# A graph layer with routed experts: other set sizes, a mean taken from a product's own sum, and a bias added as one row on TensorE

## The chip, the core and the metric

The kernel runs on one core of a Trainium2 chip. A core has five engines that run in parallel, each in the order of its own program: TensorE (PE in the profile; its weight loads are the row PEld), VectorE (DVE), ScalarE (ACT), GpSimd (POOL) and SyncE (SP). Sixteen DMA engines move data between the main memory and the on-chip memory; here SP issues the plain transfers and POOL the indirect ones, which gather or scatter rows by an index. The metric is the device time of one execution in microseconds; lower is better.

## The reference

One layer over 6,250 nodes with 256 features and 100,000 edges, all in float32:

```python
xn = _layernorm(x, axis=-1)
x = x + gnn(xn, edges, W, b, gamma, beta) + mix(xn, Wq, Wkv, Wproj, bproj)
x = x + ffn(_layernorm(x, axis=-1), gate_w, gate_b, w1, b1, w2, b2, gamma, beta)
```

`gnn` is a graph convolution: rows of `x @ W` are summed over edges with weights, normalised, and combined with its input. `mix` is linear attention with eight heads. `ffn` is a mixture of 16 experts, of which each node uses two; this is the part that the change touches:

```python
topk_vals, topk_idx = jax.lax.top_k(x @ gate_w + gate_b, 2)
topk_w = jax.nn.softmax(topk_vals, axis=-1)
h = relu(einsum('bsh,ehf->bsef', x, w1) + b1)          # 256 -> 512
expert_out = einsum('bsef,efh->bseh', h, w2) + b2      # 512 -> 256
y = x + sum(topk_w * take_along_axis(expert_out, topk_idx))
mu = mean(y); var = var(y)
return (y - mu) / sqrt(var + EPS) * gamma + beta
```

## The kernel before, in words

Nodes lie in 49 tiles of 128 (the last has 106). One long loop goes over the 782 chunks of 128 edges, a "slot" each. In a slot POOL gathers 128 rows by index (L1163), DVE writes a matrix that places them (L1167), and six slots later PE multiplies the two and so sums the edges of a tile (L1176, sums taken up at L1185). Everything else is woven into these slots by hand: `Weave` keeps pieces, Python generators, each with the slot of its next step; a step emits its instructions, and `yield n` puts the next step n slots later. The slot numbers thus fix the order of the instructions on every engine; time does not enter. After the last slot the pieces go on in the same order.

Once a pair of tiles has all its edges, `residual` makes the new `x` and the gate's logits. Tiles then go to the experts in phases, listed in `SETS` (L118): two sets, of 36 and 13 tiles, each cut into phases that end at the tile numbers given. After a phase `route` finds a slot in an expert's blocks for each token, and `scatter` lets POOL write the token's row there (L911, two per tile). A block is 128 tokens of one expert. In all but the last phase of a set only full blocks are worked on; the number that a phase counts on is a constant (`hi`, two blocks a tile less a margin), and at the set's last phase, its flush, it is `USUAL`. If the counts of the data do not bear out these constants, a flag makes the kernel do the whole expert part again (after L1194).

`expert` (L942) is one block: SP loads the first weights and the tokens, five slots later the second weights, the first bias (512 values) and the second bias `b2`, which lies in memory as a copy of 256 values for each of the 128 partitions (L965); after four more slots PE turns the tokens (L973) and ACT copies them (L977, "the xT copy"); then PE's first product (L981) and its copy to the on-chip memory (L985, "the h copy", on DVE, but on ACT in the last flush), PE's four turns (L989), ACT's four relus (L994), PE's second product `yp` (L998), DVE's addition of `b2` (L1002), and SP's store. Blocks of the first set follow each other by 8, 6 and, in its flush, 5 slots, those of the second by 4. There are four places for weights.

`combine` (L1012) works on two tiles: POOL gathers the two experts' rows of each (L1025) and ACT normalises `x` into `y` (L1029); six slots later DVE adds the two weighted rows (L1036, two products a tile) and takes mean and variance (`stats`, L312 and L313); then ACT's root and DVE's reciprocal (L318, L319), and for each tile two products and a sum give the output (L1044, L1045, L1047), which SP stores. The first set's pairs begin when its last block is stored, five slots apart; the second set's when the last block of all is stored.

Of the kernel before, what the change touches and what calls it, by code (L numbers as in the profile page):

```python
# [23 lines left out]
F32 = mybir.dt.float32  # L24
# [3 lines left out]
AF = mybir.ActivationFunctionType  # L28
OP = mybir.AluOpType
AX = mybir.AxisListType  # L30

P = 128
N = 6250
D = 256
NT = (N + P - 1) // P
# [16 lines left out]
FJ = F // P  # L52
KB = (2 * N + NE * (BLK - 1)) // BLK
WROW = 2 * F + FJ * D + FJ + D


def rows(t):
    return min(P, N - t * P)
# [56 lines left out]

SETS = ((8, 12, 16, 20, 24, 28, 32, 36), (42, 46, NT))  # L118
CUT = SETS[0][-1]
USUAL = [2 * CUT + 11, 2 * (NT - CUT) + 12]  # L120
MOST = [(2 * n + NE * (P - 1)) // P for n in (CUT * P, N - CUT * P)]
# [2 lines left out]
WA = 2 * F  # L124
# [112 lines left out]
def windowed_layer(ctx: ExitStack, tc: tile.TileContext, X, rows3, ident, loc_t, w_t, W, b, gamma, beta, wqT, wkvT, wprojT, bproj,  # L237
# [71 lines left out]
    def stats(pool, mv, src_tile):  # L309
        r = src_tile.shape[0]  # L310
        st = pool.tile([P, 6], F32, name="bnst", bufs=4)
        v.bn_stats(st[:r], src_tile)  # L312
        v.bn_aggr(mv, st[:r])  # L313

    def inv_std(pool, rs, var):
        sd = pool.tile([P, rs.shape[1]], F32, name="sd", bufs=2)
        p = rs.shape[0]
        act(sd[:p], var, AF.Sqrt, bias=eps_t[:p], scale=1.0)  # L318
        v.reciprocal(rs, sd[:p])  # L319
# [618 lines left out]
    def sync(to, source):  # L938
        issued[0] = nc.sync.dma_start(to, source).ins
        return issued[0]  # L940

    def expert(z, n, j, homes, bank, gap, copy_h):  # L942

        def row(i):
            if not loaded.get((z, i)):
                _, regs = nc.values_load_multi_w_load_instructions(
                    states[z]["rows"][0:1, i, j:min(j // 8 * 8 + 8, ends[z, j])], engines=[mybir.EngineType.SP],
                    min_val=0, max_val=(MOST[z] if i == 0 else NE - 1) * P,
                    skip_runtime_bounds_check_because="bounded by a minimum where it is computed")
                loaded[z, i] = list(regs)  # L950
            return loaded[z, i].pop(0)

        at, slots = row(1), row(0)
        wp_ = homes["w"].take()
        w = wp_()[:, :WROW]
        sync(w[:, :WA], experts[bass.ds(at, P), :WA])
        xp = homes["x"].take()
        xs = xp()
        i = sync(xs, xslots[z][bass.ds(slots, P), :])
        if n is not None:  # L960
            for m in range(n + 1, len(SETS[z])):
                tc.declare_no_dep(i, group=f"tokens{z}_{m}", reason="a full block takes no more tokens")
            tc.add_to_no_dep_group(f"loads{z}", i)
        yield gap[0]
        sync(w[:, WA:], experts[bass.ds(at, P), WA:])  # L965
        w1 = w[:, :WA].rearrange("p (c f) -> p c f", c=2)
        w2 = w[:, WA:WA + FJ * D].rearrange("p (j d) -> p j d", j=FJ)
        b1 = w[:, WA + FJ * D:WA + FJ * D + FJ]
        b2 = w[:, WROW - D:]
        yield gap[1]  # L970
        tp = bank("xtp").rearrange("p (k c) -> p k c", k=4)
        for c in range(2):
            nc.tensor.transpose(tp[:, c, :], xs[:, c * P:(c + 1) * P], ident)  # L973
        homes["x"].give(xp)
        xTp = homes["xT"].take()
        xT = xTp().rearrange("p (k c) -> p k c", k=2)
        nc.scalar.copy(xT, tp[:, :2, :])  # L977
        yield 2
        hp = bank("hp")
        for c in range(2):  # L980
            nc.tensor.matmul(hp, xT[:, c, :], w1[:, c, :], start=(c == 0), stop=(c == 1))  # L981
        homes["xT"].give(xTp)
        h_ = homes["h"].take()
        h = h_()
        copy_h(h, hp)  # L985
        yield 3
        tp = bank("htp").rearrange("p (k c) -> p k c", k=4)
        for f in range(FJ):
            nc.tensor.transpose(tp[:, f, :], h[:, f * P:(f + 1) * P], ident)  # L989
        homes["h"].give(h_)  # L990
        hTp = homes["hT"].take()
        hT = hTp().rearrange("p (k c) -> p k c", k=FJ)
        for f in range(FJ):
            act(hT[:, f, :], tp[:, f, :], AF.Relu, bias=b1[:, f:f + 1], scale=1.0)  # L994
        yield 2
        yp = bank("yp")
        for f in range(FJ):
            nc.tensor.matmul(yp[:, :D], hT[:, f, :], w2[:, f, :], start=(f == 0), stop=(f == FJ - 1))  # L998
        homes["hT"].give(hTp)
        y_ = homes["y"].take()  # L1000
        y = y_()
        v.tensor_add(y, yp[:, :D], b2)  # L1002
        homes["w"].give(wp_)
        yield 2
        before_it = issued[0]
        i = sync(yslots[z][bass.ds(slots, P), :], y)
        if n is not None:
            tc.declare_no_dep(i, group=f"stores{z}", reason="every block has rows of its own", keep=[before_it])
            tc.add_to_no_dep_group(f"stores{z}", i)
        homes["y"].give(y_)  # L1010

    def combine(ts_, homes, pool, last):  # L1012

        n = len(ts_)
        mv = pool.tile([P, n, 2], F32, name="mv", bufs=3)
        rs = pool.tile([P, n], F32, name="rs", bufs=3)
        v.memset(mv, 1.0)
        both = pool.tile([P, 2, D], F32, name="xn2", bufs=3)
        got, ys = {}, []
        for i, t in enumerate(ts_):  # L1020
            r = rows(t)
            z = 0 if t < CUT else 1
            for k in range(2):
                got[i, k] = homes["got"].take()
                nc.gpsimd.indirect_dma_start(  # L1025
                    out=got[i, k]()[:r], out_offset=None, in_=yslots[z],
                    in_offset=IndirectOffsetOnAxis(ap=slot_i[:r, t, k:k + 1], axis=0))
            y = both[:, i, :]
            act(y[:r], X[:r, t, :], AF.Identity, bias=nm2[:r, t:t + 1], scale=rs2[:r, t:t + 1])  # L1029
            ys.append(y)  # L1030
            yield 1
        yield 4
        for i, t in enumerate(ts_):
            r, y = rows(t), ys[i]
            for k in range(2):
                v.scalar_tensor_tensor(y[:r], got[i, k]()[:r], w12[:r, t, k:k + 1], y[:r], op0=OP.mult, op1=OP.add)  # L1036
                homes["got"].give(got[i, k])
            stats(pool, mv[:r, i, :], y[:r])
            yield 2
        inv_std(pool, rs, mv[:, :, 1])  # L1040
        yield 1
        for i, t in enumerate(ts_):
            r, y = rows(t), ys[i]
            v.scalar_tensor_tensor(y[:r], y[:r], mv[:r, i, 0:1], last[:r, 0, :], op0=OP.subtract, op1=OP.mult)  # L1044
            v.scalar_tensor_tensor(y[:r], y[:r], rs[:r, i:i + 1], last[:r, 1, :], op0=OP.mult, op1=OP.add)  # L1045
            o = pool.tile([P, D], F32, name="row", bufs=3)
            v.tensor_add(o[:r], y[:r], X[:r, t, :])  # L1047
            sync(out[t * P:t * P + r, :], o[:r])
            yield 2
# [59 lines left out]
    for z, phases in enumerate(SETS):  # L1109
        lo = 0  # L1110
        for n, b in enumerate(phases):
            flush = n == len(phases) - 1
            for t0 in range(a, b, 2):
                t1 = min(b, t0 + 2)
                at = max(at, min(NCH, 16 * t1 + 4) + LAG + 3)
                weave.add(at, residual(range(t0, t1)))
                last_at = at
                for t in range(t0, t1):
                    summed_at[t] = at + 3
                    if t + RING < NT and t >= 4:  # L1120
                        sum_from(t + RING)
                at += 10
            hi = USUAL[z] if flush else max(0, 2 * (b - CUT * z) - 11)
            ready = max(last_at + RES, scattered - 2)
            weave.add(ready, route(z, a, b, lo, hi, n == 0, flush))
            if flush:
                weave.add(ready + 6, token_weights(CUT * z, b))
            slow = 0 if z and flush else 1
            weave.add(ready + 2, scatter(z, n, a, b, 9, "token" if slow else "got", slow))
            scattered = ready + 11 + 2 * (b - a) * slow  # L1130
            ready += 14 + (2 * (b - a) * slow)
            for j in range(lo, hi):
                ends[z, j] = hi
                block = max(block + (4 if z else 8 if n < 3 else 5 if flush else 6), ready)
                weave.add(block, expert(z, n, j, homes, bank, (4, 3) if n < 3 and z == 0 else (5, 4),
                                        nc.scalar.copy if z and flush else v.tensor_copy))
            lo, a = hi, b
        if z == 0:
            ready_a = block + 18
# [574 lines left out]
```

## Time and profile before

| | |
|---|---|
| median of 3 runs | 1546.07 us (1545.3 to 1546.55) |
| profiled execution | 1549.07 us |
| its span, from first to last instruction | 1547.3 us |
| PE busy | 1312.2 us (85%) |
| DVE busy | 975.0 us (63%) |
| POOL busy | 967.1 us (63%) |
| ACT busy | 530.6 us (34%) |
| moved by DMA | 367.32 MB, mean 237 GB/s |

Where stretches of the span are listed, a line holds the stretch and its length, then for each engine the busy time and, in brackets, its instructions, then the granted clock of PE (1.00 is full), the mean busy share of the DMA engines, and what they moved. A line of the order of time holds start and busy time, engine, line of the code, operation, names (out<-in), sizes, and in square brackets the idle time before it and what ended that. A line of one group of instructions holds minimum, median and maximum duration in ns. The line numbers are those of the kernel before.

### The profile page before, as it was taken

To read this page: it belongs to the slowest core of one execution; us is meant where nothing else is said; L and a number is where in the kernel's file an instruction comes from. 1 tells how busy PE (TensorE), PEld (TensorE's weight loads), DVE (VectorE), ACT (ScalarE), POOL (GpSimd) and SP (SyncE) were. 2 spreads that over 40 slices of the span, in tenths; PEclk is the share of its full clock that TensorE was granted. 3 is DMA by queue.
4 is the path that set the end of the run, shared out by engine and by line. 5 is a ranking of instruction groups with operands and counts; after the bars stand their busy time and mean duration, and the time that the engine had idled before them with its cause. 6 is when DMAs were issued, how large, how long until landed. Compare 5 with 4: busy or idle time off the path is not lost. (4 is left out here: it accounts for less than half of the span.)

```text
span 1547.3 us, 22816 instructions
## 1 busy us (share of the span) xinstructions
PE 1312.2 (85%) x6144; PEld 930.1 (60%) x6144; DVE 975.0 (63%) x3338; ACT 530.6 (34%) x1417; POOL 967.1 (63%) x999
## 2 busy tenths in 40 slices
PE   4879999988768889898998989979999998788930
PEld 3836666666545567565776766757766765455620
DVE  8754444368855756757667676755565576989245
ACT  3653444423231223222332232323232335455420
POOL 1017777777777777777777777777667734753042
PEclk9999999999868989999999999999999999899975
DMA  9789933333345766677887878768878868899932
GB/s 279 260 271 376 371 103 99 103 97 115 102 159 169 242 221 224 222 258 254 275 280 234 275 258 283 233 236 287 284 241 288 289 201 317 308 378 368 361 102 70
DMA packets 180841, 367.32 MB, mean 237 GB/s; under 512 B 27091, under 2 KB 118152, under 8 KB 180694
## 3 DMA queue, kind: packets, MB, share of 16 engines
q1 hardware_dynamic: 132746, 236.69, 44.1%
q0 software_dynamic: 47712, 128.17, 26.0%
q8 instruction: 55, 0.90, 0.2%
q10 hardware_dynamic: 236, 0.80, 0.2%
q14 instruction: 92, 0.75, 0.2%
HBM read 290.00 MB, written 75.54 MB: 236 GB/s over the span
## 5 line engine op out<-in xcount | busy, mean ns | idle before, releaser
L1163 POOL DMA_INDIRECT rows<-w_hs,src_t x782 | 762.2, 975 | 354.1 <-ACT two_a L552 89.7
L1176 PE MATMUL acc<-rows,hot 128*128 128x256 f32 x1564 | 443.6, 396 | 37.4 <-DMA rows<-w_hs,src_t 31.1
L1176 PEld LDWEIGHTS acc<-rows,hot 128*128 128x128 f32 x1564 | 278.9, 195 | 129.4 <-issue 60.6
L1167 DVE TENSOR_SCALAR hot<-iota_g,loc_t,w_t 128x128 f32<-128x128 f32 x782 | 245.1, 354 | 4.0 <-PE acc L1176 4.0
L1025 POOL DMA_INDIRECT Q<-w_yslots,slot_i x98 | 99.4, 1015 | 141.8 <-issue 81.1
L994 ACT ACTIVATE hT<-htp,early 128x128 f32<-128x128 f32 x296 | 84.5, 368 | 205.6 <-issue 130.1
L998 PE MATMUL yp<-early,hT 128*128 128x256 f32 x592 | 148.2, 396 | 5.2 <-ACT hT L994 5.2
L981 PE MATMUL hp<-early,Q 128*128 128x512 f32 x296 | 143.2, 607 | 5.6 <-ACT Q L977 4.7
L998 PEld LDWEIGHTS yp<-early,hT 128*128 128x128 f32 x592 | 116.9, 198 | 32.7 <-ACT hT L994 10.8
L985 DVE COPY Q<-hp 128x512 f32<-128x512 f32 x92 | 63.4, 689 | 113.7 <-PE hp L981 113.0
L911 POOL DMA_INDIRECT w_xslots<-Q,slot_i x98 | 99.6, 1016 | 46.8 <-issue 37.1
L555 DVE SCALAR_TENSOR_TENSOR row<-two_a,two_b 128x256 f32<-128x256 f32 (+1 forms) x49 | 21.0, 430 | 132.0 <-ACT two_b L553 132.0
L549 PE MATMUL kq<-early,xnT 128*128 128x512 f32 (+1 forms) x196 | 98.5, 627 | 4.3 <-ACT xnT L545 4.3
L981 PE MATMUL hp<-Q 128*128 128x512 f32 x188 | 92.4, 615 | 10.1 <-ACT Q L977 9.1
L989 PE MATMUL htp<-ident,Q 128*128 128x128 f32 x484 | 74.7, 278 | 21.4 <-DVE Q L985 17.8
L998 PE MATMUL yp<-Q,hT 128*128 128x256 f32 x376 | 91.6, 388 | 0.4 <-ACT hT L994 0.3
L1002 DVE TENSOR_TENSOR Q<-yp,early 128x256 f32<-128x256 f32 x74 | 31.3, 423 | 95.6 <-PE yp L998 88.2
L318 ACT ACTIVATE sd<-mv,eps_t 128x2 f32<-128x2 f32 (+2 forms) x76 | 22.8, 300 | 195.5 <-DVE mv L313 191.5
L994 ACT ACTIVATE hT<-htp,Q 128x128 f32<-128x128 f32 x188 | 53.5, 367 | 94.7 <-issue 77.6
L981 PEld LDWEIGHTS hp<-early,Q 128*128 128x128 f32 x296 | 55.6, 193 | 49.1 <-issue 36.2
L998 PEld LDWEIGHTS yp<-Q,hT 128*128 128x128 f32 x376 | 72.9, 195 | 19.6 <-ACT hT L994 5.2
L1185 DVE SCALAR_TENSOR_TENSOR agg<-acc,dinv,agg 64x256 f32<-64x256 f32 x135 | 65.0, 482 | 28.6 <-PE acc L1176 25.9
(266 smaller groups left out, 1933.0 us busy)
## 6 DMA issues: line engine op xcount, KB each, us to landing
early<-in_experts SPq DMA_DIRECT2D x74, 642.0 KB
early<-in_experts SPq DMA_DIRECT2D x74, 512.0 KB
Q<-in_experts SPq DMA_DIRECT2D x47, 642.0 KB
Q<-in_experts SPq DMA_DIRECT2D x47, 512.0 KB
w_xslots<-zero_b SPq DMA_DIRECT2D x16, 1024.0 KB
w_yslots<-zero_b SPq DMA_DIRECT2D x16, 1024.0 KB
Q<-w_xslots SPq DMA_DIRECT2D x121, 128.0 KB
w_yslots<-Q SPq DMA_DIRECT2D x121, 128.0 KB
```

The source lines that it names most:

```text
L549: nc.tensor.matmul(kq[:r], xnT[:, k, :r], wkq[:, k, :], start=(k == 0), stop=(k == 1))
L911: i = nc.gpsimd.indirect_dma_start(out=xslots[z], out_offset=IndirectOffsetOnAxis(ap=slot_i[:r, t, k:k + 1], axis=0), in_=y[:r], in_offset ...
L981: nc.tensor.matmul(hp, xT[:, c, :], w1[:, c, :], start=(c == 0), stop=(c == 1))
L985: copy_h(h, hp)
L989: nc.tensor.transpose(tp[:, f, :], h[:, f * P:(f + 1) * P], ident)
L994: act(hT[:, f, :], tp[:, f, :], AF.Relu, bias=b1[:, f:f + 1], scale=1.0)
L998: nc.tensor.matmul(yp[:, :D], hT[:, f, :], w2[:, f, :], start=(f == 0), stop=(f == FJ - 1))
L1025: nc.gpsimd.indirect_dma_start(out=got[i, k]()[:r], out_offset=None, in_=yslots[z], in_offset=IndirectOffsetOnAxis(ap=slot_i[:r, t, k:k + ...
L1163: nc.gpsimd.indirect_dma_start(out=hrows[c], out_offset=None, in_=hs, in_offset=IndirectOffsetOnAxis(ap=src_t[:, c:c + 1], axis=0))
L1167: v.tensor_scalar(hots[c], iota_g[:, group_of(c) % 2, :], loc_t[:, c:c + 1], w_t[:, c:c + 1], op0=OP.is_equal, op1=OP.mult)
L1176: nc.tensor.matmul(accs[g], hots.pop(c), hrows.pop(c), start=begin, stop=end)
L1185: v.scalar_tensor_tensor(agg(t)[p0:p1], acc[p0:p1, :], dinv[p0:p1, t:t + 1], agg(t)[p0:p1], op0=OP.mult, op1=OP.add)
```

## The change

There are three edits.

The sets become 40 tiles in nine phases and 9 tiles in two, instead of 36 in eight and 13 in three. The number of blocks provided follows: 91 and 30 instead of 83 and 38, 121 in all both times. In the second set the first phase's margin grows by one, so that it counts on no block.

In the blocks of the second set only one row of `b2` is loaded, by a transfer of its own, and PE adds it to `yp` by a product of one row of ones with that row. DVE's addition becomes a copy.

In `combine` DVE's second product of a tile also writes the sum of its result. DVE scales the two sums of a pair to minus the mean; ACT takes the squares of `y` plus that, with their sum, into the place of the gathered rows; ACT's root and DVE's reciprocal follow, and the output adds minus the mean where it subtracted the mean. The statistics of DVE go, and so does the filling of `mv` with ones except for the tile that is not full.

```diff
-SETS = ((8, 12, 16, 20, 24, 28, 32, 36), (42, 46, NT))
+SETS = ((8, 12, 16, 20, 24, 28, 32, 36, 40), (46, NT))
...
-        sync(w[:, WA:], experts[bass.ds(at, P), WA:])
+        if row_b2:
+            sync(w[:, WA:WROW - D], experts[bass.ds(at, P), WA:WROW - D])
+            sync(w[0:1, WROW - D:], experts[bass.ds(at, 1), WROW - D:])
+        else:
+            sync(w[:, WA:], experts[bass.ds(at, P), WA:])
...
-            nc.tensor.matmul(yp[:, :D], hT[:, f, :], w2[:, f, :], start=(f == 0), stop=(f == FJ - 1))
+            nc.tensor.matmul(yp[:, :D], hT[:, f, :], w2[:, f, :], start=(f == 0), stop=(not row_b2 and f == FJ - 1))
+        if row_b2:
+            nc.tensor.matmul(yp[:, :D], ones[0:1, :], b2[0:1, :], start=False, stop=True)
...
-        v.tensor_add(y, yp[:, :D], b2)
+        if row_b2:
+            v.tensor_copy(y, yp[:, :D])
+        else:
+            v.tensor_add(y, yp[:, :D], b2)
...
+        minus, squares = mv[:, :, 0], mv[:, :, 1]
...
-        v.memset(mv, 1.0)
+        if rows(ts_[-1]) < P:
+            v.memset(mv, 0.0)
...
-            for k in range(2):
-                v.scalar_tensor_tensor(y[:r], got[i, k]()[:r], w12[:r, t, k:k + 1], y[:r], op0=OP.mult, op1=OP.add)
-                homes["got"].give(got[i, k])
-            stats(pool, mv[:r, i, :], y[:r])
-            yield 2
-        inv_std(pool, rs, mv[:, :, 1])
+            v.scalar_tensor_tensor(y[:r], got[i, 0]()[:r], w12[:r, t, 0:1], y[:r], op0=OP.mult, op1=OP.add)
+            v.scalar_tensor_tensor(y[:r], got[i, 1]()[:r], w12[:r, t, 1:2], y[:r], op0=OP.mult, op1=OP.add,
+                                   accum_out=minus[:r, i:i + 1])
+            homes["got"].give(got[i, 0])
+            yield 1
+        v.tensor_scalar(minus, minus, -1.0 / D, None, op0=OP.mult)
+        for i, t in enumerate(ts_):
+            r = rows(t)
+            act(got[i, 1]()[:r], ys[i][:r], AF.Square, bias=minus[:r, i:i + 1], accum_out=squares[:r, i:i + 1])
+            homes["got"].give(got[i, 1])
         yield 1
+        sd = pool.tile([P, n], F32, name="sd", bufs=2)
+        act(sd, squares, AF.Sqrt, bias=eps_t, scale=1.0 / D)
+        yield 1
+        v.reciprocal(rs, sd)
         for i, t in enumerate(ts_):
             r, y = rows(t), ys[i]
-            v.scalar_tensor_tensor(y[:r], y[:r], mv[:r, i, 0:1], last[:r, 0, :], op0=OP.subtract, op1=OP.mult)
+            v.scalar_tensor_tensor(y[:r], y[:r], minus[:r, i:i + 1], last[:r, 0, :], op0=OP.add, op1=OP.mult)
...
-            hi = USUAL[z] if flush else max(0, 2 * (b - CUT * z) - 11)
+            hi = USUAL[z] if flush else max(0, 2 * (b - CUT * z) - 11 - z)
...
                 weave.add(block, expert(z, n, j, homes, bank, (4, 3) if n < 3 and z == 0 else (5, 4),
-                                        nc.scalar.copy if z and flush else v.tensor_copy))
+                                        nc.scalar.copy if z and flush else v.tensor_copy, z == 1))
```

More of the change, by code (lines that the diff above doesn't have):

```diff
@@ L940, in sync, with expert @@
         return issued[0]
-    def expert(z, n, j, homes, bank, gap, copy_h):
+    def expert(z, n, j, homes, bank, gap, copy_h, row_b2=False):
         def row(i):
```

## The prediction

> **What bounds the kernel now.** I read the page's slices first, to see which engine is full when; then busy times by stretch, cut at events of the trace; then the order of time of VectorE (DVE), TensorE (PE) and ScalarE (ACT) inside a stretch.
>
> ```profile
> core 0: us, PE busy (x) PEld busy (x) DVE busy (x) ACT busy (x) POOL busy (x), PEclk, DMA share, GB/s
> 1035.90:1259.90 224.00, 214.06 (x965) 158.82 (x966) 132.44 (x428) 67.95 (x201) 144.35 (x149) 0.98 0.81 275
> 1259.90:1302.40 42.50, 39.09 (x178) 25.96 (x177) 26.14 (x96) 18.39 (x55) 18.32 (x19) 1.00 0.73 260
> 1375.50:1402.60 27.10, 24.16 (x91) 15.47 (x90) 24.73 (x70) 14.89 (x44) 16.48 (x16) 0.94 1.03 384
> 1433.50:1484.60 51.10, 49.35 (x203) 32.73 (x202) 8.75 (x24) 25.67 (x74) 0.00 (x0) 1.00 0.79 285
> 1490.00:1533.80 43.80, 0.00 (x0) 0.00 (x0) 37.59 (x104) 6.60 (x16) 24.82 (x24) 0.50 0.38 110
> 1533.80:1547.30 13.50, 0.00 (x0) 0.00 (x0) 0.01 (x1) 0.00 (x0) 0.00 (x0) 0.50 0.12 23
> ```
>
> Up to 1260 us (last edge product) PE is full. From 1260 to 1302 PE works off blocks and the last residuals, before the first combine product. Then set 0's combine and the blocks run together, and DVE (24.7 of 27.1 us) and DMA (share 1.03) are both full. From 1433 to 1485 only blocks are left: PE again. From 1490 the last 13 tiles' combine is DVE's alone. The last 13.5 us hold the check of the block counts and the end, and do not change.
>
> A combine pair, in order of time on DVE and ACT, and the squares with an accumulator that the kernel makes at its start:
>
> ```profile
> 1506.20 1.00 DVE L1036 SCALAR_TENSOR_TENSOR xn<-Q,w,xn 128x256 f32<-128x256 f32 x2
> 1507.23 0.43 DVE L312 BATCH_NORM_STATS2 bnst<-xn 128x6 f32<-128x256 f32 x1
> 1507.69 0.18 DVE L313 BATCH_NORM_AGGREGATE mv<-bnst 128x2 f32<-128x6 f32 x1
> 1508.29 0.17 DVE L319 RECIPROCAL rs<-sd 128x2 f32<-128x2 f32 x1 [0.42 <-ACT sd L318]
> 1508.39 0.48 DVE L1044 SCALAR_TENSOR_TENSOR xn<-xn,mv,par 128x256 f32<-128x256 f32 x1
> ...
> 1508.90 0.48 DVE L1045 SCALAR_TENSOR_TENSOR xn<-xn,rs,par 128x256 f32<-128x256 f32 x1
> 1509.42 0.42 DVE L1047 TENSOR_TENSOR row<-xn,X 128x256 f32<-128x256 f32 x1
> 1509.76 1.00 DVE L1036 SCALAR_TENSOR_TENSOR xn<-Q,w,xn 128x256 f32<-128x256 f32 x2
> ```
>
> ```profile
> L420 ACT ACTIVATE unread<-X,minus x32: 492/493/510, 35.8 to 61.8; 128x256 f32<-128x256 f32 x32
> L420 ACT ACTIVATION_READ_ACCUMULATOR unread<-X,minus x32: 185/187/193, 36.2 to 62.2; 128x1 f32 x32
> ```
>
> The starts give the steps: two products 1.03 us, statistics 0.46 + 0.10, output (L1044 to L1047) 1.37. Between the second tile's aggregate and the reciprocal DVE waits 0.42 us for ACT's root. A pair takes 6.53 us here and 6.75 beside the blocks (27.1 us for four pairs and five blocks). A block on PE alone takes 4.45 us (L981 starts at 1441.94 and 1446.39).
>
> **What the Trainium skill says.** "VectorE: DVE Perf Modes", section "Two Vector instructions with no wait between them": an op that also writes out its accumulator is two instructions. No DVE row of before has one; ACT's rows above do. "TensorE: Matmul & The Clock Gate", section "Why this matters for your kernels": a K=32 matmul takes as long as a K=128 one. The trace agrees: the 3-row bias matmul (L599) holds PE 0.21 us, one record of a 128-row float32 product 0.22. The same page, section "Architectural detail: the array is 16× 32×32, not 1× 128×128", calls ACT and DVE strict FIFO; so what stands between a square and its root in program order delays the root. The rows above keep program order.
>
> **The change, part by part.**
>
> Do the block counts still hold? Counting the reference's own routing: 90 blocks for the first 40 tiles (91 provided), 26 for the last nine (30 provided), 64 full at tile 36 (61 needed), 6 at tile 46. So the second pass stays unused, as before.
>
> (a) Main loop. By the order of the pieces, 76 instead of 81 blocks are added by the last edge sum. Five blocks are 5 x 4.45 = 22 us of PE. But the five are missing as a hole of 22 steps between the first set's last two phases. There POOL's gathers (0.95 + 0.30 us each) and the eight scatters of the moved flush (1.28 each) bound it: some 16 gathers beyond those already buffered, 20 us, plus 10, against 15 us of PE work, so 15 us of PE stand idle. 22 - 15 = 7; before's PE idles 10 of 224 us anyway, and part of that goes: **-10** (bounds 0 and -22).
>
> (b) From the last edge sum to the first combine product: 6 blocks before (the 82nd to the 87th), 17 now (77th to 93rd). 11 x 4.45 = 49, two row products 0.9, and the first gathers, which must wait for set 0's last store, 1.5: **+51.5** (42.5 becomes 94). DMA covers it: one block is 1.44 MB, 325 GB/s at that pace, below the 384 seen.
>
> (c) Set 0's combine beside blocks. Before: 17 intervals between first products of pairs, 1302.4 to 1429.5, 127.1 us. Now 19. One pair, on DVE's order: product 0.51; product with its accumulator read 0.61 (the read is not in the trace; from nothing, if it hides under the next op, to ACT's own 0.19; I take 0.1, which is ACT's step from one accumulated op to the next less the 0.40 or so of the op alone); the pair before's second output 1.37; product and accumulated product 1.16; scaling of the mean to the next step 0.17 + 0.04; then ACT: two squares, 0.49 from start to start and 0.62 to the end of the second's read, root 0.30, back to DVE 0.04; reciprocal 0.10; first output 1.38. Sum 6.8. The statistics (1.12 a pair) are gone, but 1.2 more of waiting for ACT stands in the same place. Blocks add 0.34 each on DVE; of five in four pairs, two fall into that wait: 0.25 a pair. ACT's order puts between squares and root, in turn over four pairs, nothing, an xT copy (0.35), four relus (1.14) and an h copy (0.57): 0.5 a pair. That gives **7.6** (7.0 without the insertions; 8.4 if ACT also waits for PE there). 19 x 7.6 = 144.4: **+17.3**.
> What is covered: PE needs 1.25 x (4.45 + 0.43) = 6.1 a pair, the 0.43 being the row product's two float32 passes; DMA 1.25 x 1.31 + 0.79 = 2.43 MB, 6.4 us at 384 GB/s; ACT 5.1; SP 8.25 issues at 0.58, 4.8. All are below 7.6. The row's load is one more issue right behind that of w2, eleven slots ahead of its use; if it came late, PE's next products would stand behind it. So the 3.8 MB of b2 no longer loaded (10 us of DMA), the 30 small loads that take their place and the copy for the add cost and bring nothing here. Without cover, DMA's share of the gain would be 0.4 us a pair.
>
> (d) From the last pair's first product to set 1's first: 60.5 before, with some 12 blocks still to come. Now four: the pair's own start 2.5, three blocks at 4.9, last store and gather 5.4 as before: 22.6, **-37.9**.
>
> (e) The bare combine: 43.8 for 13 tiles. Now nine: a first pair limited by its gathers (1.25 each) 7.5, three at 6.8, the single tile 5.1: 33, **-10.8**.
>
> (f) At the start one more fill of 1 MB, in front of a stretch (70 to 80 us) in which DMA stands idle; 24 memsets fewer on DVE. Nothing.
>
> Sum: -10 + 51.5 + 17.3 - 37.9 - 10.8 = +10.1. The profiled execution took 1549.07, 1547.3 of it span; the runs' median is 1546.07, 3.0 below. Predicted span 1557.4, and in runs 1546.07 + 10.1 = **1556**.
>
> **Rivals.**
> 1. *The round trip to ACT is covered* (other side). If roots come back early, the pair is bound by DMA, 6.4: 19 x 1.2 less, 1533. For it: DVE's work alone falls to some 5.5 a pair. Against it: DVE's order has nothing between scaling and reciprocal but a copy. It decides from a pair below 7.07 (10.1 / 19 under 7.6).
> 2. *ACT comes late*: stuck behind the mean, it holds xT and h back, PE falls behind, and DVE meets the lag at the copy of yp. Pair 8.4: 1571. For it: ACT and PE already wait for each other there (L981 behind the xT copy, 15.5 us). Against it: PE needs 6.1 of 7.6.
> 3. *The main loop gives back all of five blocks*: 22 instead of 10, 1544, about the same. For it: PE is busy 214 of 224 us. Against it: the hole.
> 4. *The counts fail* and the second pass runs: 128 blocks x 4.45 + 49 tiles x 3.4, some 740 us. Against it: the counts above.
>
> **How the numbers follow.** My case (pair 7.3 to 8.0, 1550 to 1564) 0.52; rival 1 0.15; 2 0.17; 3 0.15, of which 0.04 faster, 0.08 same, 0.03 slower; 4 0.01. Faster by over 0.2% (3.1 us, about what a measurement can tell): 0.19; same 0.08; slower 0.73. The range, 1541 to 1574, holds my case, most of 2 and 3 and the upper part of 1.
>
> **What would show it.** (a) 76 blocks' sums before the last edge product, which ends near 1250. (b) First combine product near 1344. (c) Starts of pairs 7.6 apart, DVE idle 1.5 to 2.5 us before each reciprocal, released by the root; DMA share under 0.95. (d) Last block's copy near 1506. (e) 33 us of bare combine. Wrong if pairs follow at under 7.07, or if the edge loop ends before 1240.

## The result, and the profile after

The changed kernel takes 1575.03 us (median of four runs, 1573.07 to 1576.04) against 1546.31 for the kernel before beside it: 1.0177 times as long, 95% interval 1.0155 to 1.0198. I had forecast 1556 and a range up to 1574; the sign was right, the size was not. The profiled execution took 1575.47, with a span of 1573.7 against 1547.3. So 26.4 us more have to be found in the trace.

I cut both profiles at five events: last edge product, first combine product, first product of set 0's last pair, first product of set 1, last output. These are the busy times of the changed kernel in the first three stretches.

```profile
core 0: us, PE busy (x) PEld busy (x) DVE busy (x) ACT busy (x) POOL busy (x), PEclk, DMA share, GB/s
1035.90:1241.00 205.10, 193.68 (x866) 144.08 (x866) 126.91 (x418) 63.50 (x177) 139.64 (x144) 0.97 0.76 258
1241.00:1352.80 111.80, 94.27 (x378) 60.57 (x378) 42.49 (x150) 37.40 (x114) 22.51 (x23) 0.95 0.73 247
1352.80:1499.90 147.10, 127.49 (x468) 74.62 (x467) 97.55 (x287) 88.98 (x275) 75.08 (x75) 0.97 0.91 307
```

Set beside the sum of the prediction (the last stretch goes from set 1's first product to the end of the span):

| stretch | before | predicted | after | after less predicted |
|---|---|---|---|---|
| up to the last edge product | 1260.1 | 1250 | 1241.0 | -9 |
| to the first combine product | 42.3 | 94 | 111.8 | +17.8 |
| to the last pair of set 0 | 127.1 | 144.4 | 147.1 | +2.7 |
| to the first product of set 1 | 60.5 | 22.6 | 29.7 | +7.1 |
| to the end | 57.3 | 46.5 | 44.1 | -2.4 |

Two rows carry the miss. In the second stretch PE is busy 94.3 of 111.8 us and nothing else is full: VectorE works 42 us, the DMA share is 0.73. So something keeps PE waiting there, where I had it full: 7.8 us for VectorE's copy of h (11 times) and 7.1 us for ACT's relus (10 times). The work itself was counted right: 75 blocks' sums are added before the last edge product and 93 before the first combine product, against 80 and 87 before. In order of time, with the waits in brackets, one round of that stretch in the changed kernel:

```profile
1324.06 1.88 PE L986 MATMUL hp<-early,Q 128*128 128x512 f32 x4
...
1325.97 0.69 DVE L990 COPY Q<-hp 128x512 f32<-128x512 f32 x1 [1.29 <-PE hp L986]
...
1326.72 0.66 PE L994 MATMUL htp<-ident,Q 128*128 128x128 f32 x4 [0.79 <-DVE Q L990]
...
1327.21 0.38 PE L978 MATMUL xtp<-ident,Q 128*128 128x128 f32 x2
1327.46 1.14 ACT L999 ACTIVATE hT<-htp,early 128x128 f32<-128x128 f32 x4 [4.26 <-issue]
...
1327.88 1.99 PE L1003 MATMUL yp<-early,hT 128*128 128x256 f32 x8 [0.29 <-ACT hT L999]
...
1329.71 1.88 PE L986 MATMUL hp<-Q 128*128 128x512 f32 x4
```

PE makes the first product (hp, 1324.06) and its next instruction is the turn of the same block's h (htp), so it stands until VectorE has copied h; then little more than the turn of the next block's tokens (xtp) lies ahead of yp, which needs ACT's relu. Every step waits for the one before: hp to hp takes 1329.71 - 1324.06 = 5.65 us, where I had put 4.45. That figure came from this round of before (PE in order of time):

```profile
1441.94 1.98 PE L981 MATMUL hp<-early,Q 128*128 128x512 f32 x4
1443.77 1.89 PE L998 MATMUL yp<-Q,hT 128*128 128x256 f32 x8
1445.49 0.38 PE L973 MATMUL xtp<-ident,Q 128*128 128x128 f32 x2
1445.71 0.60 PE L989 MATMUL htp<-ident,Q 128*128 128x128 f32 x4
1446.39 1.98 PE L981 MATMUL hp<-Q 128*128 128x512 f32 x4
```

Here the previous block's yp and the next block's xtp stand between hp and its htp, and PE never waits.

With no blocks beside it, the new combine is as fast as the old one. A pair of the stretch in which only the combine runs:

```profile
1536.97 0.48 DVE L1048 SCALAR_TENSOR_TENSOR xn<-Q,w,xn 128x256 f32<-128x256 f32 x1
...
1537.48 0.48 DVE L1049 SCALAR_TENSOR_TENSOR xn<-Q,w,xn 128x256 f32<-128x256 f32 x1
1537.89 0.08 DVE L1049 DVE_READ_ACCUMULATOR xn<-Q,w,xn 128x1 f32 x1
1537.89 0.48 DVE L1065 SCALAR_TENSOR_TENSOR xn<-xn,mv,par 128x256 f32<-128x256 f32 x1
...
1542.04 0.17 DVE L1062 RECIPROCAL rs<-sd 128x2 f32<-128x2 f32 x1 [1.49 <-ACT sd L1060]
...
1543.49 0.48 DVE L1048 SCALAR_TENSOR_TENSOR xn<-Q,w,xn 128x256 f32<-128x256 f32 x1
```

It takes 6.52 us, as before's 6.53. The read of the accumulator is there (0.08), but the next instruction starts with it at 1537.89: the product with accumulator takes 0.41 to the next start, the one without 0.51. Where the scaling of the mean follows, which needs the sum, it is 0.53.

Beside the blocks it is another matter. Set 0's pairs follow at 6.8, 6.5, 6.8 and then 10.1 or 11.8 us. One long pair of the changed kernel, in order of time on all three engines:

```profile
1466.80 0.51 ACT L1056 ACTIVATE Q<-xn,mv 128x256 f32<-128x256 f32 x1 [2.38 <-DVE mv L1053]
...
1467.31 0.49 ACT L1056 ACTIVATE Q<-xn,mv 128x256 f32<-128x256 f32 x1
...
1467.80 0.35 ACT L982 COPY Q<-xtp 128x256 f32<-128x256 f32 x1
...
1468.20 1.98 PE L986 MATMUL hp<-early,Q 128*128 128x512 f32 x4 [1.25 <-ACT Q L982]
...
1469.82 0.48 DVE L1048 SCALAR_TENSOR_TENSOR xn<-Q,w,xn 128x256 f32<-128x256 f32 x1
...
1472.58 0.42 DVE L1010 COPY Q<-yp 128x256 f32<-128x256 f32 x1 [1.75 <-PE yp L1005]
...
1476.53 1.11 ACT L999 ACTIVATE hT<-htp,early 128x128 f32<-128x128 f32 x4
...
1477.53 0.30 ACT L1060 ACTIVATE sd<-mv,eps_t 128x2 f32<-128x2 f32 x1
...
1477.86 0.17 DVE L1062 RECIPROCAL rs<-sd 128x2 f32<-128x2 f32 x1 [2.36 <-ACT sd L1060]
...
1479.93 0.47 DVE L1048 SCALAR_TENSOR_TENSOR xn<-Q,w,xn 128x256 f32<-128x256 f32 x1
```

ACT stands 2.38 us at the squares until VectorE has the mean. Behind the squares stands a block's copy of xT (1467.80), which could have been made earlier; PE's hp waits for it, the block's second product is late, and VectorE, between the two tiles of its next pair, waits 1.75 us for that product. In the same pair four relus stand between squares and root. The circle closes on VectorE itself: what it is late with is what makes it wait.

The last blocks show the row product's price, in order of time on PE in the changed kernel:

```profile
1510.48 1.98 PE L986 MATMUL hp<-Q 128*128 128x512 f32 x4
1512.30 1.89 PE L1003 MATMUL yp<-early,hT 128*128 128x256 f32 x8
1514.12 0.69 PE L1005 MATMUL yp<-early,ones 1*128 1x256 f32 x2
1514.74 0.44 PE L978 MATMUL xtp<-ident,Q 128*128 128x128 f32 x2
...
1515.64 1.98 PE L986 MATMUL hp<-early,Q 128*128 128x512 f32 x4
```

PE waits for nothing, and hp follows hp at 5.16 us. Without the row product the same place of the same kernel takes 4.39 (e8_after_norow, below): the row costs 0.77, where I had put 0.43.

### The profile page after: what moved, and what is told of

The parts are those of the page before. It is cut to its first block, busy times and chain, and to the rows that moved or that the text cites. A ratio compares the mean times of both kernels' runs of the same rounds, so it can differ in the third digit from the quotient of the medians.

```text
span 1573.7 us, 23069 instructions
## 1 busy us (share of the span) xinstructions
PE 1342.6 (85%) x6202; PEld 941.6 (60%) x6202; DVE 950.4 (60%) x3282; ACT 555.0 (35%) x1516; POOL 964.3 (61%) x999
## 4 chain that ended last, share of the span: by engine, by line
PE 44%; DVE 17%; issue 10%; DMA 8%; ACT 4%; POOL 1%; SPq 0%; POOLq 0%; ACTq 0%; DVEq 0%
PE acc L1197 13%; PE yp L1003 9%; PE hp L986 8%; DMA rows<-w_hs,src_t 4%; PE hp L667 3%; PE mix L683 2%; DMA w_xslots<-Q,slot_i 2%; PE kq L549 2%; PE htp L994 1%; DVE hot L1188 1%; PE tp L638 1%; DVE agg L1206 1%; DVE Q L990 1%; ACT Q L1056 1%; DMA Q<-w_yslots,slot_i 1%
## 5 line engine op out<-in xcount | busy, mean ns | idle before, releaser
L1003 PE MATMUL yp<-early,hT 128*128 128x256 f32 x592 | 151.6, 402 | 9.2 <-ACT hT L999 9.1
L1003 PEld LDWEIGHTS yp<-early,hT 128*128 128x128 f32 x592 | 120.2, 205 | 38.6 <-ACT hT L999 15.2
L986 PE MATMUL hp<-Q 128*128 128x512 f32 x188 | 95.6, 633 | 11.9 <-ACT Q L982 11.7
L555 DVE SCALAR_TENSOR_TENSOR row<-two_a,two_b 128x256 f32<-128x256 f32 (+1 forms) x49 | 21.1, 431 | 130.2 <-ACT two_b L553 130.2
L1003 PEld LDWEIGHTS yp<-Q,hT 128*128 128x128 f32 x376 | 70.6, 190 | 25.0 <-ACT hT L999 13.6
L994 PEld LDWEIGHTS htp<-ident,Q 128*128 128x128 f32 x484 | 57.9, 141 | 41.2 <-DVE Q L990 31.5
L982 ACT COPY Q<-xtp 128x256 f32<-128x256 f32 x121 | 45.4, 375 | 101.1 <-PE xtp L978 100.7
```

## The experiments

e1 to e4 and e9 to e12 ran on chips where the kernel before itself takes 1773 to 1777 us. In their profiles the last edge product comes at 1440 to 1462 us instead of 1240 to 1260, and one or two odd intervals, of up to 22 us, fall into the first pairs of the combine. So of those runs only ratios and the steady intervals behind the main loop are used.

For the others, the stretches of the table above, each from its own profile (e5_after is the changed kernel again):

| run | last edge product | to first combine product | to last pair of set 0 | to set 1 | to the end | span |
|---|---|---|---|---|---|---|
| before | 1260.1 | 42.3 | 127.1 | 60.5 | 57.3 | 1547.3 |
| e5_after | 1241.7 | 111.6 | 147.5 | 29.7 | 45.0 | 1575.5 |
| e13_sets | 1246.5 | 110.5 | 130.2 | 22.5 | 45.4 | 1555.2 |
| e14_row | 1254.4 | 45.2 | 128.4 | 70.2 | 57.8 | 1556.0 |
| e15_combine | 1257.1 | 42.2 | 140.4 | 63.9 | 56.8 | 1560.3 |
| e6_sets_order | 1239.6 | 96.9 | 132.6 | 22.7 | 44.8 | 1536.6 |
| e7_after_root | 1250.7 | 108.9 | 145.1 | 30.5 | 44.7 | 1579.9 |
| e8_after_norow | 1242.2 | 112.2 | 146.4 | 26.0 | 44.0 | 1570.9 |
| e16_order_late | 1242.5 | 96.6 | 131.3 | 26.7 | 45.2 | 1542.2 |

The first column varies by several us between profiles of kernels whose main loops hold the same work (e7_after_root and e5_after differ by 9), so a few us of it say nothing; the other columns repeat better.

**The sets alone** (e1_sets, and the same kernel again as e13_sets).

```diff
-SETS = ((8, 12, 16, 20, 24, 28, 32, 36), (42, 46, NT))
+SETS = ((8, 12, 16, 20, 24, 28, 32, 36, 40), (46, NT))
-            hi = USUAL[z] if flush else max(0, 2 * (b - CUT * z) - 11)
+            hi = USUAL[z] if flush else max(0, 2 * (b - CUT * z) - 11 - z)
```

> The kernel before with only the new sets (40 and 9 tiles, the second in two phases) and its minus-z in the count of blocks; the old combine and the old add of the second bias. Theory A (the order of the steps sets the pace of set 0's last blocks): in the stretch from the last edge sum to the first combine product blocks follow at 5.6 us also without the row product, so the stretch stays near 110 us as in the changed kernel; against before: main loop -19, this stretch +68, set 0's combine at 6.75 a pair (19 x 6.75 = 128, +1), last set-0 pair to first set-1 product 27 (-33), bare combine 31 (-13): +4, about 1550. Theory B (I only mis-sized the work: the row product or the new combine's ACT work slows those blocks): blocks at 4.45 there, the stretch 90, and the kernel near 1530, faster than before.

> The new sets alone, the same kernel as e1_sets. If the stages that e1_sets showed (blocks at 5.7 until the first combine product, pairs at 6.5 to 7.2 after it) stand on a chip that grants TensorE its clock: main loop -19, stretch to the first combine product +66, 19 intervals at 6.9 (131, +4), to set 1's first product 22.5 (-38), bare combine -12: about +1, 1547 to 1553. Of this the other order takes 10 to 15 (e6_sets_order had 1538). If the sets alone are nearer the changed kernel (over 1560), the loss is theirs and not the combine's.

Measured: e1_sets 1.0058 times before (1.0024 to 1.0092); e13_sets 1556.94, 1.0059 times (1.0042 to 1.0076). In order of time, e13_sets after its last edge product:

```profile
1318.13 1.88 PE L981 MATMUL hp<-early,Q 128*128 128x512 f32 x4
...
1320.05 0.69 DVE L985 COPY Q<-hp 128x512 f32<-128x512 f32 x1 [1.29 <-PE hp L981]
1320.79 0.66 PE L989 MATMUL htp<-ident,Q 128*128 128x128 f32 x4 [0.78 <-DVE Q L985]
...
1321.96 2.00 PE L998 MATMUL yp<-early,hT 128*128 128x256 f32 x8 [0.29 <-ACT hT L994]
1323.79 1.88 PE L981 MATMUL hp<-Q 128*128 128x512 f32 x4
```

The same round with the same waits, 5.66 us from hp to hp, in a kernel with the old combine and no row product. So the slow blocks come with the sets, and need neither of the other parts. Under the combine the same kernel's pairs take 6.85 on average, where the changed kernel's take 7.74. My expectation of 1547 to 1553 was low by four: the edge loop gave 13.6 here, not 19.

**Another order of steps in set 0's last blocks** (e4_after_order and e10_after_order on the changed kernel, e6_sets_order on the sets alone). A block's steps (turn of the tokens, first product, turn of h, second product) are planned 9, 11, 14 and 16 slots after its start, and set 0's last blocks are planned five slots apart. Modulo five that is 4, 1, 4, 1: one block's turn of h and the next one's turn of tokens fall into one slot, one block's second product and the next one's first into another, and nothing falls between a block's first product and its own turn of h. With 8, 10, 14 and 16 it is 3, 0, 4, 1, and the previous block's second product and the next one's turn of tokens fall between. Set 1's blocks, four slots apart, have 1, 3, 2, 0: they have those two steps in between, and from them I had the 4.45.

```diff
         nc.scalar.copy(xT, tp[:, :2, :])
-        yield 2
+        yield mid[0]
...
         copy_h(h, hp)
-        yield 3
+        yield mid[1]
...
-                weave.add(block, expert(z, n, j, homes, bank, (4, 3) if n < 3 and z == 0 else (5, 4),
+                weave.add(block, expert(z, n, j, homes, bank, (4, 3) if n < 3 and z == 0 else (5, 3) if z == 0 and flush else (5, 4),
...
```

Here mid is (2, 4) for set 0's last blocks and (2, 3), as it was, for all others.

> The changed kernel, but set 0's last blocks take their steps in another order: the turn of the tokens and the first product one slot earlier, the turn of h and the second product where they were, so that on PE the second product of one block and the turn of the next one stand between a block's first product and its own turn of h. Theory A: blocks in the stretch from the last edge sum to the first combine product follow at 4.5 to 4.7 instead of 5.66, 15 of them: -15 to -18, about 1559, and the stretch 95 instead of 112. Rival B (late weights or tokens, or VectorE's copy of h itself): they still follow at 5.5 or more and the time stays within 3 us of 1575.

> The changed kernel with the other order of steps for set 0's last blocks, the same kernel as e4_after_order, to see it where TensorE is granted its clock. Theory A: blocks follow at 4.4 to 5.0 from the last edge sum to the first combine product, that stretch 93 instead of 108, the combine's pairs as in the changed kernel: -12 to -18, about 1561. Rival B: the edge loop, whose PE work also changes its order, gives it back: within 4 us of 1576.

> The kernel before with the new sets and with the other order of steps for set 0's last blocks (turn of the tokens and first product one slot earlier); old combine, no row product. Theory A: main loop -19 against before, the stretch from the last edge sum to the first combine product 17 blocks at 4.6 = 80 to 95 instead of 42 (+45), last set-0 pair to first set-1 product -33, bare combine -13: -12 to -20 against before, 1527 to 1535, so the sets by themselves are a gain once the blocks keep their pace. Rival: the sets move work without removing any; the sum of the stages stays within 4 us of before.

Measured: e4_after_order 1.0037 times before (1.0011 to 1.0063) and e10_after_order 1.0018 (0.9995 to 1.0040), both on the slower chips, where most of these blocks follow at 4.4 to 5.3 us and the combine's long pairs stay (10.1 and 11.8). e6_sets_order takes 1538.21, 0.9932 times before (0.9911 to 0.9952): a gain of 11 us, a little less than the 12 to 20 that I expected. Against e13_sets the stretch to the first combine product falls from 110.5 to 96.9. What PE does now is seen in e16_order_late below. The rivals for this stretch, late weights or VectorE's copy of h by itself, would have kept the pace at 5.5.

**The combine alone** (e3_combine, again as e15_combine): the diff's part within `combine`, nothing else.

```diff
-            stats(pool, mv[:r, i, :], y[:r])
-            yield 2
-        inv_std(pool, rs, mv[:, :, 1])
...
+        v.tensor_scalar(minus, minus, -1.0 / D, None, op0=OP.mult)
...
+            act(got[i, 1]()[:r], ys[i][:r], AF.Square, bias=minus[:r, i:i + 1], accum_out=squares[:r, i:i + 1])
...
+        act(sd, squares, AF.Sqrt, bias=eps_t, scale=1.0 / D)
```

> The kernel before with only the new combine; old sets, old add. 17 intervals beside blocks at 7.74 instead of 7.47 (+4.5) if the changed kernel's pair holds, PE falling behind by what stands behind the squares; the bare combine 6.5 a pair as before, less the memset and the statistics: 0 to -1. Theory C (blocks that wait behind squares on ACT are late afterwards): the stretch after the last set-0 pair stays at 60 or grows: +4 to +10, about 1553. Rival (the combine by itself is no loss, pairs only get longer where more blocks stand under them): -2 to +2.

> The new combine alone, the same kernel as e3_combine: one pair in four 9 to 11 instead of 7.2, since ACT stands at the squares with a block's copy of xT behind them; 17 intervals at 7.3 to 7.9 in steady state, +5 to +10, the bare combine -0 to +1: 1552 to 1560. If the pairs are no longer than before's when only old blocks stand beside them: within 4 us of before.

Measured: e3_combine 1.0093 times before (1.0065 to 1.0121); e15_combine 1561.86, 1.0087 times (1.0068 to 1.0107). The 17 intervals grow from 127.1 to 140.4, their steady round is 6.8, 6.5, 6.8 and 10.9. So the long pair comes with the combine, whatever the sets. The bare combine gives back 0.5.

**The root behind the squares, and the squares a slot later** (e7_after_root and e9_after_late, both on the changed kernel). They tell apart which of ACT's two orders matters: what stands between squares and root, or what stands behind the squares.

```diff
 e7_after_root
             homes["got"].give(got[i, 1])
-        yield 1
         sd = pool.tile([P, n], F32, name="sd", bufs=2)
         act(sd, squares, AF.Sqrt, bias=eps_t, scale=1.0 / D)
-        yield 1
+        yield 2
 e9_after_late
         v.tensor_scalar(minus, minus, -1.0 / D, None, op0=OP.mult)
+        yield 1
         for i, t in enumerate(ts_):
...
             homes["got"].give(got[i, 1])
-        yield 1
         sd = pool.tile([P, n], F32, name="sd", bufs=2)
```

> The changed kernel, but the root is issued right behind the two squares on ACT, so that no relu or copy of a block can stand between them; the reciprocal on VectorE stays in its slot. Theory D (insertions between squares and root make one pair in four 10 to 12 us long): all pairs of set 0's combine at 6.5 to 7.0, 19 x 0.9 = -14 to -17, about 1559. Rival E (the relus are only shifted behind the root; PE's second product and VectorE's copy of it wait as long): pairs stay at 7.5 or more, within 4 us of the changed kernel.

> The changed kernel, but the two squares are issued one slot later on ACT, together with the root, so that the block's copy of xT (or h) that is issued in that slot stands ahead of the squares instead of behind them; the scaling of the mean and the reciprocal stay in their slots. Theory F (ACT stands at the squares until VectorE has the mean, some 2.4 us; the copy of xT behind it is late, so are PE's first and second product, and VectorE then waits for the second product at its copy of yp: one pair in four takes 10 to 12): all pairs 6.5 to 7.2, 19 intervals in 126 to 135 instead of 147, so -12 to -20, about 1560. Rival: the wait moves on to the reciprocal, which now comes sooner behind the squares' end, and pairs stay at 7.6: within 4 us of 1576.

Measured: e7_after_root 1578.35, 1.0181 times before (1.0148 to 1.0213), the changed kernel's own ratio; its pairs follow at 6.6, 6.5, 6.7 and 10.8. My theory D fell: with the root first, the relus come behind it, and PE's second product waits for them (1.91 us in one long pair). e9_after_late (1.0055 times before, 1.0021 to 1.0089, on a slower chip) has 6.5, 6.5, 6.7 and 7.8. e7 and e9 both put squares and root together and differ only in the slot; so it is the early slot of the squares, with a block's work behind them on ACT, that makes the long pair. The old root stood two slots behind the second tile's products; the squares stand one slot behind them, and e9 puts them where the old root was. With both orders mended (e16_order_late) the same is seen on a chip like the first one.

**Both mends** (e16_order_late: the changed kernel with the edits of e4_after_order and e9_after_late).

> The changed kernel with both mends, the other order of steps for set 0's last blocks (-12 to -15) and the squares one slot later (-12 to -16): 1545 to 1552, which leaves 8 to 14 over e6_sets_order for the row product (4 in the last blocks, the rest in the pairs) and for what is left of the combine. If it stays over 1560, one of the two mends gives its gain back to the other's stage, and the loss has another cause.

Measured: 1544.40, 0.9967 times before (0.9953 to 0.9982), a little better than I expected. First the last blocks of set 0, before the combine, in order of time:

```profile
1317.31 1.98 PE L986 MATMUL hp<-early,Q 128*128 128x512 f32 x4
...
1319.13 1.89 PE L1003 MATMUL yp<-Q,hT 128*128 128x256 f32 x8
1319.34 0.69 DVE L990 COPY Q<-hp 128x512 f32<-128x512 f32 x1 [2.29 <-PE hp L986]
1320.86 0.38 PE L978 MATMUL xtp<-ident,Q 128*128 128x128 f32 x2
...
1321.08 0.60 PE L994 MATMUL htp<-ident,Q 128*128 128x128 f32 x4
...
1321.76 1.98 PE L986 MATMUL hp<-Q 128*128 128x512 f32 x4
```

PE waits for nothing: hp is followed by the other block's yp while VectorE copies h, and hp follows hp at 1321.76 - 1317.31 = 4.45 us, with the copy of h on VectorE (in the round of before it is on ACT). In the whole stretch PE waits 1.6 us for relus and not at all for the copy of h. Then a pair beside the blocks:

```profile
1439.68 0.16 DVE L1053 TENSOR_SCALAR mv<-mv 128x2 f32<-128x2 f32 x1
1439.69 0.37 ACT L982 COPY Q<-xtp 128x256 f32<-128x256 f32 x1 [2.13 <-PE xtp L978]
1439.96 0.51 ACT L1057 ACTIVATE Q<-xn,mv 128x256 f32<-128x256 f32 x1
...
1440.12 1.99 PE L986 MATMUL hp<-early,Q 128*128 128x512 f32 x4
```

The copy of xT stands ahead of the squares, and hp starts with no wait; in the two pairs before this one hp still waits 0.7 and 0.9 us for a copy behind the squares. Over set 0's pairs VectorE's wait for yp at its copy falls from 24.6 us in the changed kernel to 7.1, while its wait for the root stays (23.1 and 20.8). Against e5_after the two mends take 15.0 us from the stretch to the first combine product and 16.2 from set 0's pairs: 31 of the 33 us by which the spans differ.

**The row product** (e2_row, again as e14_row: the row product alone; e8_after_norow: the changed kernel without it; e12_row128: with 128 rows, which adds the bias 128 times over, so it serves for the price alone).

```diff
 e2_row, e14_row: before with the change's edits in expert() and z == 1 at its call; e8_after_norow:
-                                        nc.scalar.copy if z and flush else v.tensor_copy, z == 1))
+                                        nc.scalar.copy if z and flush else v.tensor_copy, False))
 e12_row128:
-        if row_b2:
-            sync(w[:, WA:WROW - D], experts[bass.ds(at, P), WA:WROW - D])
-            sync(w[0:1, WROW - D:], experts[bass.ds(at, 1), WROW - D:])
-        else:
-            sync(w[:, WA:], experts[bass.ds(at, P), WA:])
+        sync(w[:, WA:], experts[bass.ds(at, P), WA:])
...
-            nc.tensor.matmul(yp[:, :D], ones[0:1, :], b2[0:1, :], start=False, stop=True)
+            nc.tensor.matmul(yp[:, :D], ones, b2, start=False, stop=True)
```

> The kernel before with only the row product for set 1's second bias (and its shorter load); old sets, old combine. If a row product costs PE 0.71 us, as read in the changed kernel: set 1 has 42 blocks here, of which some 12 follow each other on PE alone (+0.71 x 12 = 8.5) and 5 stand in the stretch before the first combine product (+3); those under the combine are hidden: +9 to +13, about 1557. If it costs the 0.43 that I predicted: +5 to +7, about 1552. If the rest is hidden and the DMA saved counts: 0 or below.

> The row product alone, the same kernel as e2_row: blocks on PE alone at 5.2 instead of 4.45, some 10 after the last set-0 pair (+7 to +9) and 4 before the first combine product (+3): +9 to +13, 1556 to 1560. If DVE's lighter copy and the 10 us of transfers saved pay for it: within 4 us of before.

> The changed kernel without the row product: set 1's second bias loaded whole and added by VectorE as before. If a row product costs PE 0.71: the blocks without edge products and combine beside them (two or three in the first stretch, three in the last) give back 0.71 each, and where PE holds the pair under set 0's combine up to 25 x 0.7 more: -4 to -18; blocks there in the last stretch at 4.45 instead of 5.17. If DMA (1.44 instead of 1.31 MB a block) or VectorE is what those stretches wait for, no gain or a loss of up to 8.

> The changed kernel, but the row product is made with all 128 rows of a matrix of ones and the whole second bias (loaded whole), so the bias is added 128 times over and the output differs from the reference by 127 times the second bias. If the 0.71 us of the row product is that of the one-row form (the array's rows change between 128 and 1 at its start and end), a block on PE alone comes back to 4.45 + 0.43 = 4.88 us, in the last three blocks; if every product of 256 columns costs that much at this place, it stays at 5.17.

Measured: e2_row 1.0080 times before (1.0052 to 1.0109); e14_row 1561.65, 1.0108 times (1.0077 to 1.0139), its last ten blocks at 5.22 us where before's follow at 4.45. There PE is alone, and the stretch to set 1 grows from 60.5 to 70.2. e8_after_norow 1572.57, 1.0159 times before (1.0123 to 1.0196): in the changed kernel only a few blocks stand on PE alone. Its median is 4 us under e5_after's, less than the runs tell apart; in the profiles the stretch to set 1 is 3.7 us shorter. There, without the row product:

```profile
1509.96 1.98 PE L986 MATMUL hp<-Q 128*128 128x512 f32 x4
...
1514.35 1.98 PE L986 MATMUL hp<-early,Q 128*128 128x512 f32 x4
```

The end of e12_row128, with 128 rows, in order of time:

```profile
1727.88 1.98 PE L982 MATMUL hp<-Q 128*128 128x512 f32 x4
1729.70 1.89 PE L999 MATMUL yp<-early,hT 128*128 128x256 f32 x8
1731.43 0.59 PE L1001 MATMUL yp<-early,ones 128*128 128x256 f32 x2
1731.86 0.38 PE L974 MATMUL xtp<-ident,Q 128*128 128x128 f32 x2
...
1732.71 1.98 PE L982 MATMUL hp<-early,Q 128*128 128x512 f32 x4
```

Hp follows hp at 4.83 us, against 4.39 without the product and 5.16 with one row (5.16 on this run's own chip too, in e9_after_late). So the 0.43 was right for a product with 128 rows, and the one-row form costs 0.33 more: 0.28 from yp to the next turn of tokens (1.82 + 0.62 against 1.73 + 0.43), the rest behind it.

**The new combine with both mends and without the row product** (e11_best: e6_sets_order with the new combine and the edit of e9_after_late).

> New sets and the other order of steps as in e6_sets_order (1538), with the new combine whose squares and root are issued one slot later, and without the row product. VectorE's work of a pair is then some 5.5 plus waits, PE 1.25 x 4.45 = 5.6 and the transfers 1.25 x 1.44 + 0.79 MB = 2.6 MB, 6.8 at 384 GB/s: if transfers or PE are the bound then, pairs 6.5 to 6.9 instead of 6.98 and -2 to -8 against e6, about 1533; if VectorE still waits for the root in every pair, pairs 7.2 and +4, 1542.

Measured: 0.9924 times before (0.9898 to 0.9950), on a slower chip; its steady pairs are 6.5, 6.5, 6.7 and 7.2 to 8.4. e6_sets_order, with the old combine, had 0.9932. Whether the new combine, once mended, is better than the old one isn't told by these runs; both beat before.

**The control** (e5_after).

> The changed kernel itself, as a control beside the others on the same chip: where TensorE and the transfers are granted as in the first profiles, 1575; where they are not (the kernel before then takes some 1770), its blocks still follow at 5.6 to 5.7 us from the last edge sum to the first combine product, and its ratio to the kernel before is nearer 1.

Measured: 1576.49, 1.0182 times before (1.0156 to 1.0208).

## Why the prediction was wrong, step by step

**(a) The main loop: right in sign, too small.** I had PE idle for 15 us in the hole between set 0's last two phases and took -10; this profile gave -19. PE's busy time from 1035.9 fell from 214.2 to 193.7, by five blocks of 4.1; its idle time rose only from 10 to 11.4. The hole is there: at 1090 us two blocks' first products stand 35 us apart, as they do in both kernels at about 1000. But PE idles only 8 us in it (from 1060 to 1120), not 15, and most of the 6.6 us for which before's PE idles from 1120 to 1180 are gone. Of the 19, 3.6 are there at slot 500 already, ahead of the change (its matrix on VectorE starts at 826.8 in before and at 823.2 here). From slot 500 to the last edge product the profiles with the old sets take 431 to 435 us and those with the new ones 415 to 419, so the loop gave back some 15 of the 22. That lies between my -10 and rival 3's -22; rival 3's 1544 failed, since the losses elsewhere were larger.

**(b) This is the step that failed: the 4.45 us a block in "11 x 4.45 = 49".** The duration was read from set 1's blocks, which are planned four slots apart. Of the 17 blocks 15 are set 0's, five slots apart, and there the order of the steps makes one chain through PE, VectorE and ACT: 5.66 wherever nothing else stands between (nine intervals), and more where the last residuals do. In before only a couple of such blocks stood outside the edge loop, and inside it PE stood for the copy of h only once from 1000 to 1260 us; I take it that the edge products filled these waits, and that the change took that cover away. e13_sets showed the slow blocks with nothing else changed, and e6_sets_order and e16_order_late took 13.6 and 15.0 us back of the 17.8 by which the stretch was longer than forecast. The two row products took 0.6 more than their 0.9; what is left, some 2 us, the runs don't divide.

**(c) The sum was near by luck, the mechanism was wrong.** 7.6 a pair was forecast, 7.74 measured. But I had spread a wait of VectorE for the root over all pairs. Three of four take 6.5 to 6.8: the accumulated product, taken as 0.61 and 0.65 us, takes 0.41 and 0.53. The fourth takes 10 to 12, by what I had named rival 2: ACT held at the mean, blocks' copies behind it, VectorE meeting the lag at the copy of yp. I gave it 0.17 because PE needs only 6.1 us of 7.6. That was a count of busy time, and a chain of waits doesn't need a full engine. That ACT is a strict FIFO (the Trainium skill, "TensorE: Matmul & The Clock Gate", section "Architectural detail: the array is 16× 32×32, not 1× 128×128") I had applied to the root behind the relus only; the same for the copy of xT behind the squares, at which ACT stood 2.38 us in the trace, was the costlier one. Standing at a late value is not new: in e13_sets ACT stands 36.1 us at the old root and PE 19.3 us at hp for the copy behind it, and yet VectorE does not wait for yp, and pairs take 6.85. What the new combine adds is two squares of 0.51 us, a slot earlier; e9_after_late shows that the slot counts, and why the old order could bear the same wait stays open. (By the prediction's own figures, 2.43 MB at 384 GB/s are 6.3 us, not 6.4, and the parts of (b) add up to 51.4; neither matters.)

**(d) 29.7 instead of 22.6.** e13_sets has 22.5, so the step was right for the sets. The other 7 are the new combine's (26.0 with it, in e8_after_norow; the mends take 3.0 back with the row product in place, 26.7 in e16_order_late) and the row product's (29.7 with both).

**(e) 30.6 instead of 33**: pairs at 6.5 instead of 6.8, since the two accumulated products take 0.94 us together and not 1.26, and the single tile 3.8 instead of 5.1.

**The row product**, in (b) and (d): 0.77 measured for 0.43. The page that I drew on (the same, section "Why this matters for your kernels") speaks of 32 rows being as slow as 128; the three-row product of the trace is bfloat16. For one float32 row between products of 128 rows neither was a fit, and the measured number decides. Why one row is slower than 128 stays open.

Step by step over the profiles, the sets cost 7.9 us (e13_sets), the new combine on top of them 15.7 (e8_after_norow), the row product on top of those 4.6 (e5_after), each uncertain by the several us of the main loop. One by one against before they cost 0.59%, 0.87% and 1.08%; the row's share is smaller in the changed kernel, where three of set 1's blocks follow the last pair and not some twelve.

## What to carry to other kernels

A block's time on the busiest engine holds only for the order in which its steps are interleaved: before using it elsewhere, write down the order in the new place, since at another spacing the same steps can become one chain. When work that filled the gaps (here the edge products) ends, look at what then stands between a step and the one that needs it. When an instruction is moved to an in-order engine and has to wait there for a late value, price what is queued behind it, and put independent work ahead of it: one slot of delay for the squares was worth 16 us here.

## What the runs showed of the hardware

A float32 product of one row and 256 columns between products of 128 rows takes 0.77 us of PE's time per block (hp to hp 5.16 us against 4.39 without it); with 128 rows it takes 0.43 (4.83). VectorE's read of an accumulator takes 0.08 us and overlaps the next instruction's start; the accumulating scalar_tensor_tensor reaches the next start in 0.41 us against 0.51 without, and in 0.53 where the next instruction needs the sum. ACT's read takes 0.19, and two accumulated squares start 0.51 us apart (1466.80 and 1467.31).
